# Order and PSUM banks of the softmax sums in two attentions with heads of 16

## The chip, the cores and the metric

The program runs on one core of one Trainium2 chip. The metric is the time on the device in microseconds (us), the median over several executions. A core has a matrix engine (TensorE, PE in the profile; PEld are its weight loads), a vector engine (VectorE, DVE), a scalar engine (ScalarE, ACT), GpSimd (POOL) and a queue that starts transfers (SyncE, SP). Each has its own stream of instructions, and semaphores order them. Matmul results land in PSUM, which here is used as eight banks of 512 float32 values for each of 128 partitions.

## What is computed

The reference is four layers on tokens `x` of shape (2, 256, 256). Each layer has an attention over a context of 4096 tokens, an attention of the tokens among themselves, and a feed-forward block. The change touches the attention among the tokens of layers 1 and 3, both with 16 heads of 16 dimensions. For layer 1, cut to what matters:

```python
q = (jnp.einsum('btk,ok->bto', x, Wq) / scale).reshape(b, t, H, hd)
kk = (jnp.einsum('btk,ok->bto', x, Wk) / scale).reshape(b, t, H, hd)
v = jnp.einsum('btk,ok->bto', x, Wv).reshape(b, t, H, hd)
dot = jnp.einsum('bthd,bshd->bhts', q, kk)
att = jax.nn.softmax(dot, axis=-1)
out = jnp.einsum('bhts,bshd->bthd', att, v).reshape(b, t, k)
return jnp.einsum('btk,ok->bto', out, Wu) + bu
```

Layer 3 computes the same with biases and a window: keys further than 128 tokens from the query are masked out before the softmax.

## The kernel before, in words

**Units.** `SmallAttention` (line 1336) serves both layers. One unit of work is one batch entry (of 2) and one group of four heads (of 4), so `UNITS` has eight entries. A head takes 32 partitions (`HP`): its 16 dimensions, one row that carries the negated largest score, and padding. Four heads therefore fill the 128 partitions, and their matmuls run on 32 rows each (`32*128` in the profile).

**Steps of one unit.** `first_scores` (line 1451) multiplies queries by keys into two pairs of PSUM banks (`both`, line 1421; the helper also adds the window mask with four bf16 matmuls, line 1438, where there is one). VectorE then takes the largest score of each query, one reduction per pair (line 1455), into the tile `tops`. `shift_queries` (line 1463) transposes `tops` on TensorE into a bank called `top_ps` (line 1467), and VectorE adds it to the queries (line 1468), so that the next product comes out less the largest score. `scores` (line 1470) computes that product transposed, keys on the partitions, again into two pairs, and ScalarE takes the exponential of each pair (line 1475). `weigh` (line 1478) multiplies the exponentials by the values into the bank `attn_acc` (line 1485); an extra column of ones in the values makes it deliver each head's sum of exponentials as well, and ScalarE copies the result to `a` (line 1493). `Net.inverses` (line 195) brings the sums into columns by four small matmul instructions into the bank `sums` (recorded at line 180, in the helper `matmuls`), and VectorE takes reciprocals (line 201). `normalize` (line 1495) calls `Net.to_heads` (line 204), which spreads the reciprocals over the heads' partitions in the bank `den` (line 209), and VectorE multiplies `a` by it (line 1500).

**Order.** `small_attention` puts PE, DVE and ACT under an order written by hand: each runs its instructions in the order in which the program states them. The loop in `attend` (line 1405) is a software pipeline of twelve passes. Pass i handles the first scores of unit i, shift and second scores of unit i-1, weigh of unit i-3, and sums, reciprocal and normalisation of unit i-4. Passes 4 to 7 do all of it. In this text "full pass" means one of those, and "first" and "second attention" are those of layers 1 and 3.

**Banks.** The loop runs with `banks(mm=1, sc=3, acc=1)`: one bank with the tag `mm`, three pairs with the tag `sc`, one accumulator. `sums`, `top_ps` and `den` are three tiles that take the single `mm` bank in turn. The score pairs go round a ring of three. A tile that reuses a bank waits until everything that used the former tile has finished.

The helpers `inverses` and `to_heads` are also called by the attention over the context (lines 1006 and 1096), with tiles of their own.

Of the kernel before, what the change touches and what calls it, by code (L numbers as in the profile page):

```python
# [28 lines left out]
S = 256  # L29
# [41 lines left out]
class Net:  # L71
# [120 lines left out]
            nc.vector.tensor_tensor(rest, of, part, ALU.subtract)  # L192
        nc.vector.tensor_copy(outs[:, 2, ..., :n], rest)

    def inverses(self, a):

        ps = self.mm("sums")
        for qt in range(2):
            self.matmuls(ps[:, qt * NG : (qt + 1) * NG], [(a[:, qt * P : (qt + 1) * P], self.den)])
        r = self.small.tile([P, 2, NG], F32, tag="inverses", name="inverses", bufs=2)  # L200
        self.nc.vector.reciprocal(r, ps[:, : 2 * NG].rearrange("p (q g) -> p q g", g=NG))
        return r

    def to_heads(self, r):

        ps = self.mm("den")
        for qt in range(2):
            for g in range(NG):
                self.nc.tensor.matmul(
                    ps[g * HP : (g + 1) * HP, qt * P : (qt + 1) * P],  # L210
                    lhsT=r[:, qt, g : g + 1].to_broadcast([P, HP]),
                    rhs=self.ident,
                    start=True,
                    stop=True,
                )
        return ps[:, :S]
# [105 lines left out]
    def self_attention(self, work, qT, kT, v_of, oT, mask=None, causal=False, gates=None, before=None, negated=None):  # L322
# [98 lines left out]
        with self.tc.manual_schedule(engines=by_program):  # L421
            if before is not None:
                before(0)
            for n in range(len(items) + 5):
                if before is not None and n % 4 == 1 and n // 4 + 1 < qT.shape[1]:
                    before(n // 4 + 1)
                if n < len(items):
                    scores(n)
                if 0 <= n - 1 < len(items):
                    share(n - 1)  # L430
                if 0 <= n - 3 < len(items):
                    transpose(n - 3)
                if 0 <= n - 4 < len(items) and items[n - 4][2] == 1:
                    weigh(n - 4)
# [153 lines left out]
def run(steps, n=None):  # L588

    for _ in steps if n is None else zip(range(n), steps):  # L590
        pass


class Focus:
# [28 lines left out]
    def weigh(self, y, total, factor):  # L623


        nc = self.nc
        top, norm = (self.net.sm(NT, name=n, tag=n) for n in ("f_top", "f_norm"))
        nc.scalar.activation(y, y, AF.Ln, bias=self.eps)

        ready = self.net.sm(1, name="ready", tag="ready")  # L630
        nc.scalar.activation(ready, self.eps, AF.Exp)
        nc.gpsimd.tensor_scalar(y, y, self.power[:, 0:1], 1.0, ALU.mult, ALU.mult)
        yield
        nc.vector.tensor_reduce(top, y, AX.X, ALU.max, negate=True)
        yield
        for t in range(NT):
            nc.scalar.activation(
                y[:, t, :], y[:, t, :], AF.Exp, bias=top[:, t : t + 1], accum_out=norm[:, t : t + 1]
            )
            if t % 2:  # L640
                yield
        nc.vector.tensor_tensor(factor, total[:, 0, :], total[:, 1, :], ALU.add)
        nc.vector.tensor_scalar(factor, factor, 1.0 / D, 1e-6, ALU.mult, ALU.add)
        nc.vector.reciprocal(norm, norm)
        nc.vector.tensor_tensor(factor, factor, norm, ALU.mult)
# [134 lines left out]
class ContextAttention:  # L780
# [195 lines left out]
    def attend(self, vpool, ppool, fpool):  # L976
        net, nc, PER, LAG = self.net, self.nc, self.PER, self.LAG
        focus = net.focus
        self.vpool, self.ppool = vpool, ppool
        for _ in range(4):  # L980
            self.load_values_ctx()
        focus.start(self.layer, fpool)
        fills = self.plan()
        n = len(self.UNITS)

        ready = net.sm(1, name="ready", tag="ready")
        nc.scalar.activation(ready, net.eps5, AF.Exp)
        rankings = {}
        for g in range((n + 1) * PER + LAG + 2):
            second = g - PER - LAG  # L990
            if g < n * PER:
                self.first_scores(g // PER, g % PER)
            run(self.beginning)
            run(fills.get(g, ()))
            for kc in self.rankings.get(g, ()):
                if kc not in rankings:
                    y, _, factor = focus.chunks[kc]
                    rankings[kc] = focus.sparsify(fpool, y, factor)
                run(rankings[kc], 1)
            if 0 <= second < n * PER:  # L1000
                self.scores(second // PER, second % PER)
            focus.magnitudes_of_taken()
            if 0 <= second - 1 < n * PER:
                self.weigh((second - 1) // PER, (second - 1) % PER)
            if g in self.done:
                self.inverses = net.inverses(self.weighed)
                if self.done[g] == n - 1:
                    run(self.normalize(n - 1))
            for kc in self.weighings.get(g, ()):
                run(focus.weighing[kc], 1)  # L1010
# [73 lines left out]
    def shift_queries(self, u):  # L1084

        nc = self.nc
        ps = self.net.mm("top_ps")
        for qt in range(2):
            nc.tensor.transpose(ps[:, qt * P : (qt + 1) * P], self.tops[qt], self.net.ident)
        yield  # L1090
        nc.vector.tensor_tensor(self.q[u], self.q[u], ps[:, :S], ALU.add)

    def normalize(self, u):

        nc, out = self.nc, self.q[u]
        nc.vector.tensor_tensor(out, self.weighed, self.net.to_heads(self.inverses), ALU.mult)
        if self.v_bias is not None:
            c = self.UNITS[u][1]
            nc.vector.tensor_scalar_add(out, out, self.v_bias[:, c : c + 1])
        yield  # L1100
# [235 lines left out]
class SmallAttention:  # L1336
# [66 lines left out]
            made = []  # L1403

    def attend(self):
        n = len(self.UNITS)
        for i in range(n + 4):
            if 0 <= i - 4 < n:
                self.inverses = self.net.inverses(self.weighed[i - 4])
            if 0 <= i - 1 < n:  # L1410
                self.shift_queries(i - 1)
            if i < n:
                self.first_scores(i)
            if 0 <= i - 3 < n:
                self.weigh(i - 3)
            if 0 <= i - 1 < n:
                self.scores(i - 1)
            if 0 <= i - 4 < n:
                self.normalize(i - 4)

    def both(self, name, rows_of, columns_of):

# [37 lines left out]
                negate=True,  # L1460
            )

    def shift_queries(self, u):

        ps = self.net.mm("top_ps")
        for qt in range(2):
            self.nc.tensor.transpose(ps[:, qt * P : (qt + 1) * P], self.tops[u % 2][:, qt, :], self.net.ident)
        self.nc.vector.tensor_tensor(self.q[u], self.q[u], ps[:, :S], ALU.add)
# [9 lines left out]
    def weigh(self, u):  # L1478
        nc = self.nc
        b, c = self.UNITS[u]  # L1480
        acc, ps = self.net.acc("attn_acc"), self.weights.pop(u)
        for kt in range(2):
            for i in range(NG):
                at = (c * NG + i) * VH
                nc.tensor.matmul(
                    acc[i * HP : (i + 1) * HP, :S],
                    lhsT=self.v[:, b * 2 + kt, at : at + HP],
                    rhs=ps[i // 2][:, i % 2, kt * S : (kt + 1) * S],
                    start=kt == 0,
                    stop=kt == 1,  # L1490
                )
        self.weighed[u] = self.work.tile([P, S], F32, name="a", tag="a", bufs=3)
        nc.scalar.copy(self.weighed[u], acc[:, :S])

    def normalize(self, u):

        nc, a = self.nc, self.weighed.pop(u)
        b, c = self.UNITS[u]
        den = self.net.to_heads(self.inverses)
        nc.vector.tensor_tensor(self.oT[:, c, b * S : (b + 1) * S], a, den, ALU.mult)  # L1500


# [777 lines left out]
```

## Time and profile before

| what | before |
|---|---|
| median of 3 runs | 2547.02 us (2538.18 to 2547.83) |
| profiled execution, its own time | 2547.81 us |
| its span in the profile | 2546.1 us |
| mean granted TensorE clock | 0.953 |
| PE busy | 2346.3 us, 92% of the span |
| DVE busy | 1544.8 us, 61% |
| ACT busy | 1093.1 us, 43% |
| POOL busy | 334.3 us, 13% |

The profile is one execution. Its page gives busy time by engine, a chain of waits followed back from the end, and groups of instructions. The trace behind it gives a timeline with the start of every instruction, and windows with busy times and the granted clock. In a timeline row the columns are start and length in us, engine, line, operation, output<-input, shapes and count; the brackets hold the idle time of the engine before it and what ended that idle time. Most matmul rows are merged: `x16` is sixteen records, two for each of eight float32 matmuls. Matmuls overlap in the array, so the distance from the start of one group to the start of the next says more than a row's length.

### The profile page before, as it was taken

To read this page: it belongs to the slowest core of one execution; us is meant where nothing else is said; L and a number is where in the kernel's file an instruction comes from. 1 tells how busy PE (TensorE), PEld (TensorE's weight loads), DVE (VectorE), ACT (ScalarE), POOL (GpSimd) and SP (SyncE) were. 2 spreads that over 40 slices of the span, in tenths; PEclk is the share of its full clock that TensorE was granted. 3 is DMA by queue.
4 is the path that set the end of the run, shared out by engine and by line. 5 is a ranking of instruction groups with operands and counts; after the bars stand their busy time and mean duration, and the time that the engine had idled before them with its cause. 6 is when DMAs were issued, how large, how long until landed. Compare 5 with 4: busy or idle time off the path is not lost.

```text
span 2546.1 us, 42824 instructions
## 1 busy us (share of the span) xinstructions
PE 2346.3 (92%) x17142; PEld 1255.4 (49%) x17142; DVE 1544.8 (61%) x2719; ACT 1093.1 (43%) x1917; POOL 334.3 (13%) x505
## 2 busy tenths in 40 slices
PE   7999999999998689999999999989999986889988
PEld 3454545544544364545455444544458443455453
DVE  4978887778546548787777878343331454335252
ACT  2456555565615333655555556421131342224141
POOL 3000010000034602000010000000020121003030
PEclk9999999999999799999999999988999997798998
DMA  5432222231010134232222220201322100000100
GB/s 179 154 98 84 89 89 89 71 109 45 10 54 18 48 108 129 80 105 89 89 93 81 80 79 28 86 9 54 99 90 76 42 18 14 33 20 12 57 12 21
DMA packets 97798, 174.42 MB, mean 69 GB/s; under 512 B 15120, under 2 KB 63888, under 8 KB 96704
## 3 DMA queue, kind: packets, MB, share of 16 engines
q1 hardware_dynamic: 97600, 171.68, 21.0%
q8 instruction: 136, 2.23, 0.4%
q14 instruction: 62, 0.51, 0.1%
HBM read 154.25 MB, written 0.59 MB: 61 GB/s over the span
## 4 chain that ended last, share of the span: by engine, by line
PE 81%; DVE 9%; ACT 5%; issue 2%; POOL 1%; DMA 1%; SPq 0%; ACTq 0%; DVEq 0%; POOLq 0%
PE s L1137 11%; PE s L1113 11%; PE attn_acc L1161 9%; PE v_ps L180 6%; PE proj L180 6%; PE k_ps L1034 5%; DVE mx L1121 3%; PE f_ps L180 2%; PE kc_sum L180 2%; PE expert L180 2%; PE s L180 2%; PE c_acc L1718 2%; PE ffn_ps L180 2%; PE s L1430 2%; PE o L411 1%
## 5 line engine op out<-in xcount | busy, mean ns | idle before, releaser
L1121 DVE TENSOR_REDUCE mx<-s 128x2 f32<-128x1024 f32 x512 | 603.0, 1220 | 221.4 <-PE s L1113 218.8
L1147 ACT ACTIVATE p<-s 128x1024 f32<-128x1024 f32 x512 | 496.0, 1021 | 255.3 <-PE s L1137 253.3
L1137 PE MATMUL s<-xa_q,xa_k 32*128 32x256 f32 x4096 | 341.1, 402 | 25.9 <-DVE mx L1121 23.0
L1113 PE MATMUL s<-xa_k,xa_q 32*128 32x512 f32 x2048 | 337.7, 643 | 7.0 <-ACT p L1147 2.3
L1137 PEld LDWEIGHTS s<-xa_q,xa_k 32*128 32x128 f32 x4096 | 212.1, 184 | 167.0 <-issue 92.3
L1161 PE MATMUL attn_acc<-p,xv 128*32 128x256 f32 x4096 | 276.4, 386 | 0.7 <-ACT p L1147 0.7
L667 DVE TENSOR_TENSOR ge<-fy 128x960 bf16<-128x960 f32 (+14 forms) x240 | 169.5, 706 | 6.5
L1113 PEld LDWEIGHTS s<-xa_k,xa_q 32*128 32x128 f32 x2048 | 111.3, 183 | 124.7 <-issue 60.1
L1161 PEld LDWEIGHTS attn_acc<-p,xv 128*32 128x32 f32 x4096 | 107.4, 109 | 131.0 <-issue 84.0
L621 POOL TENSOR_TENSOR fy<-fy,low 128x256 f32<-128x256 f32 x64 | 46.4, 725 | 877.8 <-ACT fy L620 877.6
L669 DVE TENSOR_TENSOR rank<-rank,ge 128x960 bf16<-128x960 bf16 (+14 forms) x240 | 104.1, 434 | 6.0
L671 DVE TENSOR_TENSOR rank<-rank,ge 128x960 bf16<-128x960 bf16 (+14 forms) x240 | 100.7, 420 | 2.6
L387 POOL TENSOR_SCALAR p<-p,r 128x128 f32<-128x128 f32 (+1 forms) x192 | 82.5, 442 | 134.7 <-DVE r L383 77.6
L1081 ACT COPY xv<-v_ps 128x512 f32<-128x512 f32 x64 | 37.6, 587 | 131.3 <-PE v_ps L180 131.3
L368 ACT ACTIVATE p<-p,top 128x256 f32<-128x256 f32 (+1 forms) x128 | 57.1, 447 | 65.5 <-DVE top L356 63.0
L1034 PE MATMUL k_ps<-ctx_k,w_L0x_wq 128*64 128x512 f32 x256 | 68.2, 630 | 2.7 <-DMA ctx_k<-in_ctxT 2.4
L180 PE MATMUL f_ps<-f_wk,f_ctx 128*128 128x256 f32 x256 | 68.9, 400 | 0.6 <-DMA f_ctx<-in_ctxT 0.6
L1718 PE MATMUL c_acc<-pT,ctx_n 128*128 128x256 f32 x256 | 62.3, 388 | 4.2 <-ACT pT L1691 3.0
L180 PEld LDWEIGHTS f_ps<-f_wk,f_ctx 128*128 128x128 f32 x256 | 44.4, 189 | 43.3 <-issue 26.5
L180 PE MATMUL kc_sum<-f_tok,fy 128*128 128x257 f32 x256 | 64.6, 394 | 0.0
L180 PE MATMUL v_ps<-w_L0x_wv,ctx_v 128*128 128x256 f32 x256 | 63.8, 392 | 0.8 <-ACT k_dense L1047 0.8
L180 PE MATMUL expert<-h,w_L1f_eg 128*128 128x512 f32 x128 | 61.8, 604 | 2.6 <-DVE h L1552 2.6
(478 smaller groups left out, 3380.0 us busy)
## 6 DMA issues: line engine op xcount, KB each, us to landing
ctx_k<-in_ctxT SPq DMA_DIRECT2D x128, 512.0 KB
ctx_v<-in_ctxT SPq DMA_DIRECT2D x64, 256.0 KB
xa_k<-k_dense SPq DMA_DIRECT2D x512, 32.0 KB
f_ctx<-in_ctxT SPq DMA_DIRECT2D x32, 256.0 KB
f_tok<-in_ctx SPq DMA_DIRECT2D x16, 512.0 KB
ctxT<-in_ctxT SPq DMA_DIRECT2D x16, 512.0 KB
ctx_n<-in_ctx SPq DMA_DIRECT2D x16, 512.0 KB
xa_k<-key_masks SPq DMA_DIRECT2D x128, 8.0 KB
```

Source lines behind the costliest of these rows:

```text
L180: self.nc.tensor.matmul(out, lhsT=lhsT, rhs=rhs, start=i == 0, stop=i == len(pairs) - 1)
L387: nc.gpsimd.tensor_scalar(p[:, j, :nk], p[:, j, :nk], r[:, j : j + 1], 1.0, ALU.mult, ALU.mult)
L667: nc.vector.tensor_tensor(ge[:, :, :n], w[:, :, :n], w[:, :, P - n :], ALU.is_ge)
L669: nc.vector.tensor_tensor(rank[:, :, P - n :], rank[:, :, P - n :], ge[:, :, :n], ALU.add)
L671: nc.vector.tensor_tensor(rank[:, :, :n], rank[:, :, :n], ge[:, :, :n], ALU.subtract)
L1034: nc.tensor.matmul(ps[i * HR : (i + 1) * HR, :], lhsT=self.wk[:, d, c * HR : (c + 1) * HR], rhs=ctx[:, d, :], start=d == 0, stop=d == ND - 1,)
L1113: nc.tensor.matmul(pairs[i // 2][:, i % 2, :], lhsT=self.q[u][rows, qt * P : (qt + 1) * P], rhs=k[rows, :], start=True, stop=True,)
L1121: nc.vector.tensor_reduce(mx[:, qt, 2 * i : 2 * i + 2, kc], sc, AX.X, ALU.max)
L1137: nc.tensor.matmul(pairs[i // 2][:, i % 2, kk * S : (kk + 1) * S], lhsT=k[rows, at], rhs=self.q[u][rows, :], start=True, stop=True,)
L1147: nc.scalar.activation(p, sc, AF.Exp, scale=DH**-0.5)
L1161: nc.tensor.matmul(self.acc[i * HP : (i + 1) * HP, :S], lhsT=v[:, 2 * k2 + kk, at : at + HP], rhs=ps[i // 2][:, i % 2, kk * S : (kk + 1) * S],
L1718: nc.tensor.matmul(accs[m], lhsT=of[:, (k + i) % (KC // P), m * P : (m + 1) * P], rhs=pT[:, i, :], start=k + i == 0, stop=k + i == KT - 1,)
```

## The change

`shift_queries` and `normalize` no longer take an `mm` bank each. Each pass from the second on takes one `mm` bank, `aux`, and hands its right half to `shift_queries` for the transposed tops and its left half to `normalize` for the spread reciprocals. The sums no longer use an `mm` bank: `inverses` writes them into columns 256 to 263 of the accumulator bank that `weigh` has just used for the same unit.

The order within a pass changes too. `normalize` of unit i-4 moves ahead of `scores` of unit i-1. `inverses` moves from the start of the pass after to the end of the pass in which its unit was weighed, so that it works on unit i-3 instead of i-4, and its reciprocals are used in the following pass.

```diff
--- before.py
+++ after.py
@@ -192,18 +192,19 @@
             nc.vector.tensor_tensor(rest, of, part, ALU.subtract)
         nc.vector.tensor_copy(outs[:, 2, ..., :n], rest)
-    def inverses(self, a):
-        ps = self.mm("sums")
+    def inverses(self, a, ps=None):
+        ps = self.mm("sums") if ps is None else ps
         for qt in range(2):
             self.matmuls(ps[:, qt * NG : (qt + 1) * NG], [(a[:, qt * P : (qt + 1) * P], self.den)])
         r = self.small.tile([P, 2, NG], F32, tag="inverses", name="inverses", bufs=2)
         self.nc.vector.reciprocal(r, ps[:, : 2 * NG].rearrange("p (q g) -> p q g", g=NG))
         return r
-    def to_heads(self, r):
-        ps = self.mm("den")
+    def to_heads(self, r, ps=None):
+        ps = self.mm("den") if ps is None else ps
         for qt in range(2):
             for g in range(NG):
                 self.nc.tensor.matmul(
@@ -1403,20 +1404,23 @@
             made = []
     def attend(self):
         n = len(self.UNITS)
         for i in range(n + 4):
-            if 0 <= i - 4 < n:
-                self.inverses = self.net.inverses(self.weighed[i - 4])
+            aux = self.net.mm("aux") if 0 <= i - 1 else None
             if 0 <= i - 1 < n:
-                self.shift_queries(i - 1)
+                self.shift_queries(i - 1, aux[:, S:])
             if i < n:
                 self.first_scores(i)
             if 0 <= i - 3 < n:
                 self.weigh(i - 3)
+            if 0 <= i - 4 < n:
+                self.normalize(i - 4, aux[:, :S])
             if 0 <= i - 1 < n:
                 self.scores(i - 1)
-            if 0 <= i - 4 < n:
-                self.normalize(i - 4)
+            if 0 <= i - 3 < n:
+                self.inverses = self.net.inverses(self.weighed[i - 3], self.acc[:, S:])
     def both(self, name, rows_of, columns_of):
@@ -1460,9 +1464,8 @@
                 negate=True,
             )
-    def shift_queries(self, u):
-        ps = self.net.mm("top_ps")
+    def shift_queries(self, u, ps):
         for qt in range(2):
             self.nc.tensor.transpose(ps[:, qt * P : (qt + 1) * P], self.tops[u % 2][:, qt, :], self.net.ident)
         self.nc.vector.tensor_tensor(self.q[u], self.q[u], ps[:, :S], ALU.add)
@@ -1478,7 +1481,8 @@
     def weigh(self, u):
         nc = self.nc
         b, c = self.UNITS[u]
-        acc, ps = self.net.acc("attn_acc"), self.weights.pop(u)
+        self.acc = acc = self.net.acc("attn_acc")
+        ps = self.weights.pop(u)
         for kt in range(2):
             for i in range(NG):
                 at = (c * NG + i) * VH
@@ -1492,11 +1496,11 @@
         self.weighed[u] = self.work.tile([P, S], F32, name="a", tag="a", bufs=3)
         nc.scalar.copy(self.weighed[u], acc[:, :S])
-    def normalize(self, u):
+    def normalize(self, u, ps):
         nc, a = self.nc, self.weighed.pop(u)
         b, c = self.UNITS[u]
-        den = self.net.to_heads(self.inverses)
+        den = self.net.to_heads(self.inverses, ps)
         nc.vector.tensor_tensor(self.oT[:, c, b * S : (b + 1) * S], a, den, ALU.mult)
```

`first_scores`, `both`, `scores` and the projections are untouched, and the attention over the context calls `inverses` and `to_heads` as before.

## The prediction

> **What bounds the kernel now.** I read the page first. Its chain of waits, followed back from the last instruction, is mostly TensorE:
>
> ```profile
> PE 81%; DVE 9%; ACT 5%; issue 2%; POOL 1%; DMA 1%; SPq 0%; ACTq 0%; DVEq 0%; POOLq 0%
> ```
>
> Time is therefore won only where TensorE stands idle or waits inside the changed loop. The instructions that write `top_ps` place the two attentions at 1653 to 1708 us (first, no mask) and 2200 to 2263 us (second, with the window mask): about 119 us of 2546 in all. Next I read the timeline of one full pass of the first, all engines, with start, duration, instruction and, in brackets, the idle time before it and what ended it:
>
> ```profile
> 1678.13 0.44 PE L1467 MATMUL top_ps<-ident,sa_top 128*128 128x128 f32 x2 [0.30 <-DVE inverses L201]
> ...
> 1678.50 1.15 PE L1430 MATMUL s<-sa_k,sa_q 32*128 32x256 f32 x16
> ...
> 1679.57 1.07 PE L1485 MATMUL attn_acc<-p,sa_v 128*32 128x256 f32 x16
> 1679.68 2.36 DVE L1455 TENSOR_REDUCE sa_top<-s 128x4 f32<-128x1024 f32 x2 [0.65 <-PE s L1430]
> ...
> 1680.57 1.52 PE L1430 MATMUL s<-sa_q,sa_k 32*128 32x256 f32 x16
> 1680.71 0.37 ACT L1493 COPY a<-attn_acc 128x256 f32<-128x256 f32 x1 [3.07 <-PE attn_acc L1485]
> 1681.81 1.94 ACT L1475 ACTIVATE p<-s 128x1024 f32<-128x1024 f32 x2 [0.73 <-PE s L1430]
> ...
> 1682.02 0.64 PE L209 MATMUL den<-ident,inverses 128*32 128x128 f32 x16
> 1682.80 0.42 DVE L1500 TENSOR_TENSOR sa_oT<-a,den 128x256 f32<-128x256 f32 x1 [0.77 <-PE den L209]
> ...
> 1683.37 0.58 PE L180 MATMUL sums<-den,a 128*128 128x4 f32 x4 [0.70 <-DVE sa_oT L1500]
> 1683.99 0.21 DVE L201 RECIPROCAL inverses<-sums 128x8 f32<-128x8 f32 x1 [0.76 <-PE sums L180]
> 1684.25 0.20 PEld L1467 LDWEIGHTS top_ps<-ident,sa_top 128*128 128x128 f32 x2 [0.39 <-DVE inverses L201]
> ```
>
> From `top_ps` to `top_ps` a pass takes 6.12 us. TensorE waits three times in it: 0.70 us before `sums` (the single `mm` bank is still read for `sa_oT`), 0.30 us before `top_ps` (the bank is still read for the reciprocal), and inside the second scores, which take 1.45 us to the next instruction here against 1.07 us in the last pass (1699.06 to 1700.13), where no first scores are in the way. Vector (3.41 us of work) and Scalar (2.31) are not full. In the second attention the timeline gives 6.99 us a pass (2230.49 to 2237.48), with the same 0.71 and 0.30, and second scores of 1.23.
>
> **What the change does to a full pass.** It deletes no instruction: the built instruction orders have as many matmuls, reductions and copies as before, and SP and POOL issue the same DMAs in the same order. Only TensorE's and Vector's orders in these two loops change. TensorE's pass becomes tops, first scores, weigh, `den`, second scores, `sums`.
>
> Start-to-start steps in the first attention, from this timeline: tops 0.37, first scores 1.07, weigh to `den` 0.89 (1701.99 to 1702.88), `den` 0.57 (1707.80 to 1708.38, where nothing holds the successor), second scores 1.07, `sums` 0.51 (1701.48 to 1701.99). Sum **4.48 us**. The three waits go for these reasons:
> - 0.70: `sums` writes the accumulator's bank and waits only for the copy of `a`, finished 1.5 us after weigh began (1.14 to its start, 0.37 long), while `den` and second scores take until 2.5 us after it.
> - 0.30: the next tops wait for the `sa_oT` multiply, no longer for the reciprocal. Vector holds the multiply behind both reductions, which start 1.18 after first scores: with tops at 0 they end near 3.9 and the multiply at 4.35. The slack is small but positive. The reciprocal, last in Vector's pass, delays the query add behind it only where it is later than tops plus 0.48; it ends about 0.15 before that.
> - 0.38: `den` now stands between weigh and second scores, so the first reduction (ends at 2.7) has freed the bank before second scores come at 2.90.
>
> **What is late next.** The score pairs are a ring of three with four uses per pass, so the second pair of first scores reuses the bank that the previous pass's first exponential reads. In before that was free 1.8 us early. Where the ring was tight it shows:
>
> ```profile
> 2208.72 1.94 ACT L1475 ACTIVATE p<-s 128x1024 f32<-128x1024 f32 x2
> ...
> 2209.79 2.08 PE L1430 MATMUL s<-sa_k,sa_q 32*128 32x256 f32 x12 [0.45 <-ACT p L1475]
> ```
>
> TensorE goes on 0.05 us after the first exponential (1.02 each), not after the second. The loop is: second pair to weigh 1.06, weigh 0.89, `den` 0.57 (it now stands inside this loop), second scores to the exponential's start 1.24 (1699.06 to 1700.30), exponential 1.02, release 0.05: **4.83 us**. So 0.35 of the gain is given back and a pass takes 4.83, not 4.48: 1.29 less than before. In the second attention the mask matmuls add 0.54 to the step, and the exponential starts 1.57 after second scores: 1.60 + 0.89 + 0.57 + 1.57 + 1.02 + 0.05 = **5.70 us** against 6.99 (TensorE alone 5.47): again 1.29.
>
> **The clock.** The fourth full pass of the first attention took 7.31 (1690.37 to 1697.68):
>
> ```profile
> 1690.00:1694.00 4.00, 3.70 (x31) 2.02 (x34) 1.54 (x3) 0.00 (x0) 0.00 (x0) 0.57 0.00 0
> ```
>
> The column before the last two is the granted clock. The Trainium skill (TensorE: Matmul & The Clock Gate, the table of two states in Part 1) ties half speed to at least one idle window of about 3.4 us. The row disagrees: half speed came after a stretch in which no gap exceeded 0.70 us, though three gaps and the thin `sums` (4 columns) fell together. By the rule this 1.19 us would be unrelated to the change; by the row fewer gaps should keep the clock up. I follow the row and count it as gained; the ends for the range are 0 and 1.19.
>
> **Start and end of the loops.** `sums` of unit 0 moves to the end of pass 3 and is followed by tops after 0.51 instead of 0.91 (0.81 in the second): 0.40 and 0.30 gained. At the end first scores are gone, and the new wait bites: weigh follows `sums`, and the one accumulator bank is held until the reciprocal has read it. The skill's PSUM — Partial Sum Buffer (PSUM bank collisions raise a hardware error) speaks against this placement: different columns of a bank do not make two engines independent, so guard the bank. The row has weigh 0.51 after `sums`; under the rule it comes after the reciprocal, 0.62 + 0.21 + 0.05 = 0.88. The built order also makes weigh wait for Vector, so I take 0.88: 0.37 lost twice per attention, 1.5 us in all, with `den` and the copy of `a` queued behind the waiting weigh. Full passes hide this wait under tops and first scores (1.44 long); without that cover it would cost 0.37 in each of the eight, 3 us. In turn `sums` there now waits for the copy, which stands behind the two exponentials once.
>
> From tops of pass 8, first attention: second scores 1.83, `sums` 2.90, weigh 3.78, exponentials to 5.11, copy to 5.49, `sums` 5.55, weigh 6.43, copy to 7.94, `sums` 7.99, reciprocal to 8.82, `den` 8.87, projection 9.44, against 10.70 (1697.68 to 1708.38): 1.26 gained. Second attention, by the same steps with the mask: 9.76 against 11.23 (2251.46 to 2262.69): 1.47.
>
> **Sum.** First: 0.40 + (25.66 - 4 x 4.83) + 1.26 = 8.0. Second: 0.30 + (27.97 - 4 x 5.70) + 1.47 = 6.9. Together 14.9 us. Span 2546.1 becomes 2531.2; with the 1.7 outside the span (2547.81 - 2546.1) that is 2532.9, call it **2533**. The runs' median, 2547.02, is 0.8 below the profiled execution; from it the answer is 2532.1.
>
> **Rivals.**
> 1. *The exponential does not hold first scores* (pairs are handed on sooner): TensorE alone, 4.48 and 5.47, 4 x (0.35 + 0.23) = 2.3 more, 2530.6. For: 0.35 rests on a ring worked out by hand. Against: the 0.45 us row above. 0.16.
> 2. *The second exponential is the one that frees the pair*, so a pass is 1.02 longer: 8.2 given back, 2541. For: both exponentials read pairs that first scores need within a pass. Against: the same row. 0.11.
> 3. *The half clock takes over, slower than before.* Half-clock steps: first scores 2.02 and weigh 1.84 (chain, 1691.03 and 1668.27), tops 0.62, second scores 2.08, mask 0.96; `den` 1.1 is an estimate by doubling. A pass would take 8.2 or 10.1, costing 3.4 or 4.4 against my forecast. With all eight full passes at half clock: 31.2 - 14.9 = 16.3 slower, 2564. From four passes on it eats the whole gain. For: passes 1 to 3 of both attentions run at half clock (0.50 from 1654). Against: full passes of the second attention stayed at 1.00 with more idling. 0.05.
> 4. *It does not act* (a wait the order hides replaces each one removed): 2547. Against: no wait on the old `mm` neighbours is left. 0.02.
>
> **Numbers.** Forecast 0.66. About 0.5% (12.7 us) is what a measurement of this kernel can tell from no change; faster than that means under 2534.3. The forecast lies 1.4 below this line, and the three runs of before spread over 9.7 us, so I give it 0.75 of ending under it; rival 1 gets 0.85, rival 2 nearly nothing. Faster 0.64, same 0.31, slower 0.05. Range: one run of before was 9 below the median, which takes the forecast to about 2522; upward rival 2, 2541.
>
> **What would show it.** Full passes of 4.83 and 5.70, first scores about 1.4 long with a wait ended by `p`; no wait of `sums` on `sa_oT` nor of tops on `inverses`; weigh waiting for `inverses` in the last two units only; clock 1.00 throughout passes 4 to 7. It is wrong if tops wait for `sa_oT` (Vector as the bound), if passes exceed 5.4, or if half-clock stretches grow.

## The result, and the profile after

| what | before | after |
|---|---|---|
| median (lowest to highest) of 5 runs each | 2547.02 us (2538.18 to 2556.89) | 2528.74 us (2522.94 to 2530.6) |
| ratio, 95% interval | | 0.9925 (0.9902 to 0.9949) |
| span of the profiled execution | 2546.1 us | 2524.2 us |
| mean granted TensorE clock | 0.953 | 0.958 |

The whole interval lies beyond 0.5%, its near end only just: the changed kernel is faster. The chain of waits on its page is as much TensorE as before:

```profile
PE 81%; DVE 8%; ACT 5%; issue 2%; POOL 1%; DMA 1%; SPq 0%; ACTq 0%; DVEq 0%; POOLq 0%
```

The timeline of a full pass of the first attention, changed kernel, weight loads left out:

```profile
1679.27 0.41 PE L1470 MATMUL aux<-ident,sa_top 128*128 128x128 f32 x2
1679.51 0.21 DVE L202 RECIPROCAL inverses<-attn_acc 128x8 f32<-128x8 f32 x1 [0.81 <-issue]
...
1679.62 1.56 PE L1434 MATMUL s<-sa_k,sa_q 32*128 32x256 f32 x16
1679.73 0.42 DVE L1471 TENSOR_TENSOR sa_q<-sa_q,aux 128x256 f32<-128x256 f32 x1
1680.83 2.36 DVE L1459 TENSOR_REDUCE sa_top<-s 128x4 f32<-128x1024 f32 x2 [0.68 <-PE s L1434]
...
1681.11 1.07 PE L1489 MATMUL attn_acc<-p,sa_v 128*32 128x256 f32 x16
...
1682.00 0.62 PE L210 MATMUL aux<-ident,inverses 128*32 128x128 f32 x16
...
1682.55 1.15 PE L1434 MATMUL s<-sa_q,sa_k 32*128 32x256 f32 x16
1683.10 0.41 DVE L1504 TENSOR_TENSOR sa_oT<-a,aux 128x256 f32<-128x256 f32 x1
...
1683.62 0.61 PE L180 MATMUL attn_acc<-den,a 128*128 128x4 f32 x4
...
1684.09 0.42 PE L1470 MATMUL aux<-ident,sa_top 128*128 128x128 f32 x2
```

From `aux` for the tops to the next such row a pass takes 4.82 us; before it took 6.12. No PE row carries a bracket: the waits of `sums` on `sa_oT` (0.70) and of the tops on `inverses` (0.30) are gone, and the second scores are back at 1.15 long, 1.07 to the next group. What has grown is the first scores: 1.49 to the next group instead of 1.07, with no bracket because the wait lies inside a merged row. The multiply for `sa_oT` ends at 1683.51, 0.58 before the tops that need its bank.

The windows over the same passes (us, PE, PEld, DVE, ACT and POOL busy with counts, granted clock, DMA share, GB/s) show full clock in all of them:

```profile
1673.00:1677.00 4.00, 4.00 (x54) 2.73 (x58) 2.49 (x5) 1.94 (x2) 0.00 (x0) 1.00 0.00 0
1677.00:1681.00 4.00, 4.00 (x62) 2.80 (x54) 2.50 (x6) 2.31 (x3) 0.00 (x0) 1.00 0.01 4
1681.00:1685.00 4.00, 3.92 (x64) 2.56 (x66) 3.14 (x5) 1.59 (x3) 0.00 (x0) 1.00 0.00 0
```

The two traces cut at the same instructions, in us. The first pass of each loop up to its tops, 4.95 and 5.99 us in both kernels, is left out. "Full passes" runs from the tops of pass 4 to those of pass 8; "end" from there to the projection:

| stretch | before | after | gained |
|---|---|---|---|
| ahead of the first attention | 1648.50 | 1646.44 | 2.06 |
| first: tops of pass 1 to 4 | 18.57 | 13.52 | 5.05, of it 0.44 the step from `sums` to tops |
| first: full passes | 25.66 | 19.18 | 6.48 |
| first: end | 10.69 | 9.69 | 1.00 |
| between the attentions | 485.81 | 485.37 | 0.44 |
| second: tops of pass 1 to 4 | 23.31 | 22.87 | 0.44 |
| second: full passes | 27.96 | 22.69 | 5.27 |
| second: end | 11.23 | 10.04 | 1.19 |
| after it | 283.41 | 283.46 | -0.05 |

The steps that the change touches give 0.44 + 6.48 + 1.00 + 0.44 + 5.27 + 1.19 = 14.8 us. The spans differ by 21.9. The other 7.1 are 4.61 in passes 1 to 3 of the first attention, which ran at half clock before and, but for pass 1, at full clock after, with the same instructions except the moved `sums`, 2.06 ahead of the attentions, where nothing is changed, and 0.4 elsewhere. Whether these come with the change is asked below.

### The profile page after: what moved, and what is told of

The parts are those of the page before. It is cut to its first block, busy times and chain, and to the rows that moved or that the text cites. A ratio compares the mean times of both kernels' runs of the same rounds, so it can differ in the third digit from the quotient of the medians.

```text
span 2524.2 us, 42790 instructions
## 1 busy us (share of the span) xinstructions
PE 2333.7 (92%) x17142; PEld 1251.2 (50%) x17142; DVE 1545.5 (61%) x2719; ACT 1093.0 (43%) x1917; POOL 334.4 (13%) x505
## 4 chain that ended last, share of the span: by engine, by line
PE 81%; DVE 8%; ACT 5%; issue 2%; POOL 1%; DMA 1%; SPq 0%; ACTq 0%; DVEq 0%; POOLq 0%
PE s L1114 11%; PE s L1138 11%; PE attn_acc L1162 9%; PE v_ps L180 6%; PE proj L180 6%; PE k_ps L1035 5%; DVE mx L1122 3%; PE f_ps L180 3%; PE kc_sum L180 2%; PE expert L180 2%; PE s L180 2%; PE c_acc L1722 2%; PE ffn_ps L180 2%; PE s L1434 2%; PE o L412 1%
```

## The experiments

Sums over passes below are cut as in the table. Medians of the kernel before differ from one comparison to the next (2542.29, 2544.56 and 2554.46 in three of them), so times are compared only by the ratio within one.

### Each half of the change alone

The new banks, with `normalize` left behind the second scores (`inverses` goes to the start of the next pass, which by itself moves nothing):

```diff
             aux = self.net.mm("aux") if 0 <= i - 1 else None
+            if 0 <= i - 4 < n:
+                self.inverses = self.net.inverses(self.weighed[i - 4], self.acc[:, S:])
...
-            if 0 <= i - 4 < n:
-                self.normalize(i - 4, aux[:, :S])
             if 0 <= i - 1 < n:
                 self.scores(i - 1)
-            if 0 <= i - 3 < n:
-                self.inverses = self.net.inverses(self.weighed[i - 3], self.acc[:, S:])
+            if 0 <= i - 4 < n:
+                self.normalize(i - 4, aux[:, :S])
```

> Banks of the change, order of before (den after the second scores). My theory (what costs is the chain of waits on the one mm bank): sums wait for nothing, but tops now wait for the sa_oT multiply, which comes 1.2 us after den starts. Full pass of the first attention about 5.1 us (before 6.12, after 4.82), of the second about 6.0 (before 6.99, after 5.68); first scores without a wait on the exponential; second scores of the first attention again 1.45. Whole kernel about 2.5 us slower than the changed one. Rival (the place of den does the work, the banks do not): passes stay at 6.1 and 7.0. On the clock: if tops 1 to tops 3 of the first attention (same instructions in all kernels) takes 9.2 us here as in the changed kernel and 12.1 in kernels with the old banks, the new banks cause it; if it varies without regard to the banks, it is the clock's window.

The new order, with the three tiles in one `mm` bank in turn as before:

```diff
-            aux = self.net.mm("aux") if 0 <= i - 1 else None
-                self.shift_queries(i - 1, aux[:, S:])
+                self.shift_queries(i - 1, self.net.mm("top_ps"))
-                self.normalize(i - 4, aux[:, :S])
+                self.normalize(i - 4, None)
-                self.inverses = self.net.inverses(self.weighed[i - 3], self.acc[:, S:])
+                self.inverses = self.net.inverses(self.weighed[i - 3])
```

> Order of the change (den ahead of the second scores), banks of before (sums, tops and den in the one mm bank in turn). My theory: the wait of second scores on the first reduction goes, sums wait for the sa_oT multiply behind both reductions in the first attention only, and tops wait for the reciprocal (0.30) in both. Full pass about 5.3 us in the first, 5.85 in the second; no wait of first scores on the exponential in the first. Rival (the banks do the work): passes stay near 6.1 and 7.0. Clock: tops 1 to tops 3 of the first attention 12.1 us if the old banks cause the half clock there, otherwise anything from 9 to 12.

Measured, passes of the first and second attention, each within 0.1 of what was expected: banks alone 5.08 and 5.95 us, ratio 0.996 (0.9938 to 0.9982); order alone 5.25 and 5.76, ratio 0.9939 (0.9915 to 0.9963). In the timeline of banks alone the second scores still wait, inside their row, for the first reduction:

```profile
1688.52 1.52 PE L1434 MATMUL s<-sa_q,sa_k 32*128 32x256 f32 x16
```

In that of the order alone the waits on the shared bank are still there, the longer one halved because `den` now comes earlier:

```profile
1683.80 0.58 PE L180 MATMUL sums<-den,a 128*128 128x4 f32 x4 [0.35 <-DVE sa_oT L1503]
1684.42 0.21 DVE L202 RECIPROCAL inverses<-sums 128x8 f32<-128x8 f32 x1 [0.76 <-PE sums L180]
...
1684.68 0.44 PE L1469 MATMUL top_ps<-ident,sa_top 128*128 128x128 f32 x2 [0.30 <-DVE inverses L202]
```

Each half removes its own wait. By the stretches, banks alone gain 12.1 us and the order alone 11.5, yet both together 14.8 (each figure includes the 1.19 us of half clock in pass 7 before). In a pass of the first attention 1.04 and 0.87 us are gained alone and 1.30 together, 0.61 less than their sum. Of this 0.34 is the distance from the 4.48 that TensorE's work alone would take to the 4.82 that came, the loop's share if the prediction's account is right. For the other 0.27 the rows show waiting that either half shortens: the wait of `sums`, 0.70 before, goes with the banks and is 0.35 with the order alone. The loop was tried next.

### The loop through the exponential, by doubling it

The first exponential of each unit is issued twice (same result), the second once:

```diff
-            self.nc.scalar.activation(p, sc, AF.Exp, scale=self.scale)
+            for _ in range(2 - len(self.weights[u])):
+                self.nc.scalar.activation(p, sc, AF.Exp, scale=self.scale)
```

> The changed kernel with the first exponential of each unit computed twice, the second time over the same result; ScalarE is busy 3.3 us of a pass then, not full. My theory: the first exponential lies in the loop that sets the pass, so the whole 1.02 us appears: full passes of 5.85 us in the first attention and 6.7 in the second, with first scores waiting for the exponential. Rival (TensorE's own work or VectorE sets the pass, ScalarE has 2.5 us to spare): passes stay at 4.82 and 5.69.

Passes of 5.81 and 6.68 us: 0.99 longer in both attentions, for an exponential of 1.02. One execution took 2556.29 us. The merged row of the first scores breaks in two, and the timeline names the wait:

```profile
1695.28 2.99 ACT L1479 ACTIVATE p<-s 128x1024 f32<-128x1024 f32 x3 [1.11 <-PE s L1434]
...
1695.99 0.70 PE L1434 MATMUL s<-sa_k,sa_q 32*128 32x256 f32 x4
...
1697.41 1.13 PE L1434 MATMUL s<-sa_k,sa_q 32*128 32x256 f32 x12 [0.72 <-ACT p L1479]
```

The `x12` starts 2.13 after the exponentials begin: two of them and 0.1, not three. So the pass is bound by the loop, and it is the last reader of the first pair that frees the bank. Had TensorE's own work set the pass (rival 1), it would have absorbed part of the 1.02; had the second pair been the one waited for (rival 2), the wait would have ended after the third exponential, at 1698.3.

### Shortening the loop

The matmuls of the four heads run on four row groups, 32 rows of the array each, and each pair belongs to two of them. If first scores fill one pair after the other, only four matmuls stand behind the wait for the second pair instead of six:

```diff
+        two = NG // 2
+        if name == "s1":
+            steps = [(half, g * two + i) for g in range(2) for half in range(2) for i in range(two)]
```

> The changed kernel with the matmuls of the first scores issued pair by pair (all of the first pair, then all of the second) instead of half by half; the same matmuls. My theory of the loop (second pair of first scores, weigh, den, second scores, first exponential): the second pair now comes about 0.45 us later in the pass, after the first exponential has let its bank go, so the wait of 0.35 goes; but only two of four row groups run at first, so the eight matmuls take about 1.3 us instead of 1.07. Full pass of the first attention about 4.74 us (4.82 in the changed kernel), of the second about 5.7 (5.69). Rival (the 0.35 us is no wait but the cost of first scores after tops): pass longer by the 0.26 of lost overlap, 5.1 and 5.9.

```profile
1672.18 1.94 ACT L1482 ACTIVATE p<-s 128x1024 f32<-128x1024 f32 x2 [1.12 <-PE s L1438]
...
1672.83 1.56 PE L1438 MATMUL s<-sa_k,sa_q 32*128 32x256 f32 x16
...
1674.32 1.07 PE L1493 MATMUL attn_acc<-p,sa_v 128*32 128x256 f32 x16
```

The passes stayed at 4.82 and 5.69. That was expected of the second attention (5.7); in the first neither 4.74 nor the rival's 5.1 came. In the single records the second pair begins at 1673.26, 0.05 after the first exponential's end, and weigh comes 1.06 later, exactly as with six matmuls. The records also show why. Each row group of the second pair has two float32 matmuls, four records, and they start one behind another, at 1673.26, 1673.58, 1673.80 and 1674.01; in the changed kernel they start at 1680.05, 1680.37, 1680.58 and 1680.80, just as far apart. The two matmuls that were moved belong to the other pair's row groups and ran beside them, so taking them out of the loop made it no shorter. The run also serves as a control: with the same full passes as the changed kernel its ratio is 0.9897 (0.9868 to 0.9927) against 0.9925. A total here does not resolve 3 us; the stretches do.

### `den` out of the loop

In full passes, `normalize` directly behind the tops:

```diff
                 self.shift_queries(i - 1, aux[:, S:])
+            if 0 <= i - 4 and i < n:
+                self.normalize(i - 4, aux[:, :S])
             if i < n:
...
-            if 0 <= i - 4 < n:
+            if 0 <= i - 4 < n and i >= n:
                 self.normalize(i - 4, aux[:, :S])
```

> The changed kernel with den (and the sa_oT multiply) moved again: in the full passes directly behind the tops, ahead of the first scores; the last passes keep the changed order. My theory has two loops that pull against each other: den between first and second scores lengthens the loop over the exponential by 0.57 us, and without it second scores come before the first reduction has freed their bank. First attention: the loop over the exponential falls to 4.4 us, TensorE alone is 4.48, but second scores wait about 0.3, so 4.8 (4.82 in the changed kernel): no gain. Second attention: loop 5.2, TensorE 5.47, second scores wait under 0.1, so 5.5 (5.69). Rival (the exponential's loop is the only one): 4.5 and 5.47.

It came out the other way: 5.49 and 6.17 us a pass, ratio 0.9964 (0.994 to 0.9988). The timeline shows what was overlooked:

```profile
1686.45 0.41 PE L1472 MATMUL aux<-ident,sa_top 128*128 128x128 f32 x2
...
1686.91 0.42 DVE L1473 TENSOR_TENSOR sa_q<-sa_q,aux 128x256 f32<-128x256 f32 x1
...
1687.38 0.64 PE L210 MATMUL aux<-ident,inverses 128*32 128x128 f32 x16 [0.52 <-DVE sa_q L1473]
...
1690.04 1.52 PE L1436 MATMUL s<-sa_q,sa_k 32*128 32x256 f32 x16
```

`den` starts 0.05 us after the add to the queries, although that add reads the other half of the `aux` bank: the program guards the bank as one tile. Whether the chip could have run both at once was not tried. And with `den` no longer between weigh and second scores, these wait for the first reduction again (1.52 long). In the changed kernel `den` comes 2.7 us after the tops, when the add is long over. No version better than the changed kernel came out of the two attempts.

### What repeats of the clock

The two kernels again, unedited, one execution each:

> The kernel before once more. Full passes at full clock 6.12 and 6.99 us as in the first profile. Theory that the half clock in passes 1 to 3 of the first attention is a matter of where the clock's 3.4 us windows fall: tops 1 to tops 3 differs from 12.1 us, or some other stretch does. Rival that it belongs to this kernel: 12.1 us again.

> The changed kernel once more. Full passes 4.82 and 5.68 us. Theory of the clock's window: tops 1 to tops 3 of the first attention may be anything from 9 to 12 us. Rival that the change shortens it: 9.2 us again.

And the kernel before twice more:

> The kernel before a third time, for the clock. If its gaps bring the clock down, one half-clock stretch should again lie in passes 4 to 7 or the last passes of the first attention (both profiles of before had one, none of the kernels with fewer gaps did): passes 4 to 7 plus last passes 36.3 to 36.8 us. If it is chance, 35.1 to 35.2.

> The kernel before a fourth time, for the same: 36.3 to 36.8 us from tops of pass 4 to the projection with a half-clock stretch, about 35.1 without.

| run | span | first: tops of pass 1 to 3 | 3 to 4 | full passes + end | half clock in |
|---|---|---|---|---|---|
| before | 2546.1 | 12.11 | 6.46 | 36.36 | passes 1 to 3, 7 |
| before_again | 2550.8 | 12.10 | 6.22 | 36.78 | passes 1 to 3, end |
| before_third | 2546.3 | 12.10 | 6.48 | 36.36 | passes 1 to 3, 7 |
| before_fourth | 2546.8 | 12.10 | 6.47 | 36.37 | passes 1 to 3, 7 |
| after | 2524.2 | 9.16 | 4.36 | 28.87 | pass 1 |
| after_again | 2525.1 | 12.10 | 5.55 | 28.68 | passes 1 to 3 |

These executions took 2552.53 and 2526.77 us (again), 2548.02 and 2548.47 (third and fourth). The window that replaces pass 7's stretch in the second profile of before, then one of the changed kernel's passes 1 and 2 in its own second profile:

```profile
1705.00:1709.00 4.00, 4.00 (x38) 1.94 (x42) 0.42 (x1) 0.37 (x1) 0.00 (x0) 0.57 0.01 4
```

```profile
1655.00:1659.00 4.00, 4.00 (x26) 2.65 (x30) 1.45 (x2) 1.94 (x2) 0.00 (x0) 0.50 0.00 0
```

Two things come apart here. The half clock late in the first attention, apart from the one at its start, is in all four profiles of before (in pass 7 three times, in the end once). Of the other profiles only the one with the doubled exponential has it (in pass 4, at 1685 to 1689 us), and there TensorE waits 0.72 us in every pass again. The two of the changed kernel and the four of the other edits have none.

The half clock in passes 1 and 2 is in the changed kernel as well: 12.10 us in its second profile. So most of the 4.61 us there is no steady gain of the change. It doesn't follow the banks either: tops 1 to 3 took 11.23 with the new banks alone and 11.23 with the old banks in the new order. The second profile of before was expected to differ from 12.1 there if the placing of the clock's windows decides; it did not, and the late stretch moved instead.

Waits alone do not decide it: full passes of the second attention before have the same waits (0.71 and 0.30) at full clock, and the first attention with `den` directly behind the tops kept full clock in its full passes too, with waits of 0.52 and 0.37. The records show what does. In these traces the half clock comes in whole windows of 3.41 us: the stretch in pass 7 is one of them, 1690.43 to 1693.84, and the one at the start of that loop is five, 1652.88 to 1669.95. For each window, add up the work of the array: for every matmul record the share of the 128 x 128 array that it uses, times the values streamed through it, counted twice for float32 (on one row group a float32 record of 256 values follows the last after 0.21 us; a bf16 mask matmul of 256 values after 0.11). The fullest windows hold about 8,200. Over the whole of all eleven profiles:

| work in a window | windows | next window at half clock |
|---|---|---|
| under 2,950 | 668 | 658 |
| 2,950 to 3,150 | 85 | 45 |
| over 3,150 | 7,136 | 0 |

The window ahead of the half clock in pass 7 held 2,965 (2,956 and 2,964 in the third and fourth profile; in the second, ahead of the one in the end, 2,790), and 2,696 with the doubled exponential, so the half clock returned where waiting was put back. The least in full passes of the changed kernel was 4,857 (4,773 in its second profile), and in the second attention before, where the mask matmuls add work, 4,161. So waits count by the work that they take out of a window, and where the windows fall on the passes decides which one drops below the limit. The busy share of TensorE doesn't tell: the third half-clock window of before_again was 100% busy with 3,040, and the next stayed at half clock.

At the start of the loop the third half-clock window held 2,957 to 3,040 in the four profiles of before and the clock stayed at half; it held 3,005 and 3,002 with banks alone and order alone, and the first one 3,021 in the first profile of the changed kernel, and full clock came back. These lie at the limit, so that 12.1, 11.2 and 9.2 us there are the placing of the windows rather than a gain.

In the second pair of spans (before_again and after_again), the two attentions account for 60.05 + 68.50 - 51.29 - 61.58 = 15.7 of 25.7; the work ahead of them, unchanged, differs by 11.2. Totals of single executions carry that much noise.

## Why the prediction was right

- **The full passes.** 4.83 and 5.70 us were worked out; 4.82 and 5.69 came. The gain was put at 6.34 and 5.17 and measured 6.48 and 5.27. Part of this is that pass 4 of the first attention began shorter, at 4.73.
- **The three waits** went for the reasons given, and banks alone and order alone show two of them returning each with its own part. The slack put at the multiply for `sa_oT` was small but positive; it measured 0.58. The reciprocal came closer than thought: it was to end 0.15 before the query add could start, and ended 0.01 before it (1679.72 and 1679.73).
- **The loop that gives 0.35 back.** Doubling the exponential lengthened a pass by 0.99, and ended the wait on the exponential that was named. This rules out rivals 1 and 2. Its term "second pair to weigh" came at 1.06 as taken; that it is four records in a row on each row group, and not a count of matmuls, was learnt from the run that fills pair by pair. The wait itself is 0.42, not 0.35: first scores take 1.49 to the next group instead of 1.07, while tops, `den` and `sums` took 0.35, 0.55 and 0.47, together 0.08 less than in the sum of 4.48.
- **The start of the loops.** 0.40 and 0.30 predicted, 0.44 and 0.44 measured.
- **The end of the loops** is where a size was off: 9.44 and 9.76 us predicted, 9.69 and 10.04 measured. In the first attention's end:

```profile
1684.09 0.42 PE L1470 MATMUL aux<-ident,sa_top 128*128 128x128 f32 x2
1684.32 0.21 DVE L202 RECIPROCAL inverses<-attn_acc 128x8 f32<-128x8 f32 x1 [0.81 <-issue]
...
1684.59 1.07 PE L1489 MATMUL attn_acc<-p,sa_v 128*32 128x256 f32 x16
...
1687.10 0.61 PE L180 MATMUL attn_acc<-den,a 128*128 128x4 f32 x4
...
1687.80 0.21 DVE L202 RECIPROCAL inverses<-attn_acc 128x8 f32<-128x8 f32 x1 [1.22 <-PE attn_acc L180]
...
1688.06 1.07 PE L1489 MATMUL attn_acc<-p,sa_v 128*32 128x256 f32 x16 [0.36 <-DVE inverses L202]
```

  The wait of weigh on the reciprocal is there, 0.36 and 0.35 in the last two units, as the Trainium skill (PSUM — Partial Sum Buffer, PSUM bank collisions raise a hardware error) led me to take it: the program guards the bank as a whole, and no run here leaves the guard out. But the reciprocal came 0.70 after the four `sums` matmuls began, not 0.62, so weigh came 0.96 after them, not 0.88; and in pass 8 weigh came 0.50 after the tops, not 0.37, because the same reciprocal was still due. The first scores, which cover this in full passes, are gone there.
- **The clock.** The 1.19 us of half clock in pass 7 were counted as gained, on the row alone. That held: four profiles of before had such a stretch, the two of the changed kernel none, and the least work in a window of its full passes, 4,773, is far from the 3,000 or so at which the clock drops. The reason given, that three gaps and the thin `sums` fell together, comes near this; the measure, work in a window, was not known then.
- **The sum.** 8.0 + 6.9 = 14.9 predicted; 7.9 + 6.9 = 14.8 in the stretches. The medians differ by 18.3 us, in an interval of 13 to 25 us by the ratio. The rest above 14.8 is not shown to be the change's. That the time fell at 2528.74 rather than 2533 rests on such parts, not on a step of the working, and so, in part, does the interval's clearing 12.7 us: that was luck.
- **Rivals 3 and 4.** The clock was 1.00 in all full passes after, and the passes are 1.3 shorter.

## What to carry to other kernels

When a wait is removed from a software pipeline, look for the loop that closes next through the ring of buffers, and add it up from start-to-start steps of the old trace: here it gave a pass within 0.01 us. Two parts of a change that remove different waits in one pass do not add up (12.1 and 11.5 made 14.8), since they share waits and meet the same next limit. A bank shared between two uses is as good as two banks only where the other use is over by then; move an instruction past that cover and the wait is back, 0.52 us here. A thin loop can also lose clock: count the array's work in a window, not the time that TensorE is busy.

## What the runs showed of the hardware

- The clock of a 3.41 us window followed the array's work in the window before it: half after 658 of 668 windows with under 2,950 (of about 8,200 at most), full after all 7,136 with over 3,150, whether the window itself ran at half or full clock. The Trainium skill (TensorE: Matmul & The Clock Gate, Part 1) ties half clock to an idle window of about 3.4 us; the length agrees, the idleness does not: in before no gap of TensorE in that loop exceeded 0.70 us. Why ten of the 668 kept full clock stays open.
- Float32 matmuls of 32 rows ran side by side on the row groups and one behind another on each: four records on a group took 1.06 us to the next instruction whether two groups were at work or four, and all eight matmuls on four groups 1.07.
- Repeated profiles of the same kernel differ by some 9 us ahead of the attentions (1648.03 to 1657.14 for before), in instructions that no version here touches.
